# Residual of an attention block added by TensorE and evicted by ScalarE, in a fused attention and state-space kernel

## The chip, the cores and the metric

The kernel runs on one NeuronCore of one Trainium2 chip. The metric is the device time of one execution in microseconds (us). Before the change three runs gave 9474.05, 9482.28 and 9482.04 us, with a median of 9482.04 us. The profiled execution is a further one, with a time of its own.

The engines are TensorE (PE in the profile; PEld is its weight load), VectorE (DVE), ScalarE (ACT), GpSimd (POOL) and SyncE, whose queue (SP) issues nearly all transfers.

## The reference, cut to what matters

The input `x` has 8 images of 256 channels and 48 x 48 = 2304 positions. Two layers follow each other, both with a residual:

```python
# layer 0: attention over the 16 most similar positions
feat, pos = split(groupnorm(x)_tokens @ W.T + bias)          # 256 and 256 columns
pos = pos / max(norm(pos), 1e-12)
sim = pos @ pos.T                                            # 2304 x 2304 per image
topksim, topkid = top_k(sim, 16)
out = sum_k softmax(topksim)_k * feat[topkid_k]
x = x + out

# layer 1: two stacked selective scans ("mamba", depth 2) over the 2304 positions
for i in range(2):
    xn = layernorm(h);  xi, z = split(xn @ in_w.T)           # 512 and 512
    xc = silu(causal_conv4(xi));  dt, B, C = projections(xc)
    h_t = h_{t-1} * exp(dt_t * A) + dt_t * B_t * xc_t        # 512 channels x 16 states
    y = (sum over states of h_t * C_t + xc * D) * silu(z)
    h = y @ out_w.T
x = x + h
```

The change concerns the line `x = x + out` of layer 0, and the order of the work around it.

## The kernel before, in words

All arithmetic is in 32-bit floats. The program's order on each engine is the order in which the Python code emits instructions: it is written by hand, in timetables, and each engine works through its own list in that order.

**The scan sets the clock.** Layer 1 cuts an image into 6 chunks of 384 positions; 6 chunks x 2 depths make 12 *units* per image, 96 in all. A unit has 16 *steps* (32 channels each), and a step two halves of two states, so 32 halves per unit and 3072 in all. The main loop at the end of the function runs over these halves, `m`. In each half ScalarE makes the next half's decays (`decay`, L917, two exponentials into one of two PSUM banks), and VectorE runs the recurrence as one scan instruction (`run_scan`, L932). Every second half GpSimd forms the scan's input two steps ahead (`make_bx`, L893), and multiplies the states of the step before by C (`pool_part`, L960).

**SHARE** says for each half whether GpSimd ("G") or VectorE ("V", an extra product at L934) multiplies the states by C. It has three rows: row 0 for units 1 to 9 of an image, row 1 for units 0, 10 and 11, row 2 for the last image. A half marked V writes its states into the PSUM bank, and ScalarE saves the last state (`carry`, L948).

**Timetables.** Everything else of a unit stands in tables of (place, function, arguments), where place counts halves from the unit's start. Functions of the table `between` are emitted ahead of the half's scan, those of `behind` after it. These two serve units 1 to 9, `between_spare` and `behind_spare` units 0, 10 and 11, and a third pair the last image. Which pair serves an entry is decided by where the entry's place falls.

**Attention rides along.** While image b is scanned, the attention of image b+1 is emitted a piece per half, behind everything else (`ahead.go`). Only the first image's attention runs alone, ahead of the scan. Attention works on 18 blocks of 128 rows. A block follows the table `within`, with a new block every 16 halves: products `similar` (L444), copies to SBUF (`keep_similar`, L453), the four top-16 passes of VectorE (`top`), masked weights turned by TensorE and exponentiated (L495 to L504), the weighted sum (`weigh`, L515), its division (`average`, L522), a transposition back to channels (`turn_back`, L531), and the residual (`finish`, L539). `turn_back` and `finish` stand at the same place, 24 of the block, which falls on places 14 and 30 of a unit. With every third block a chunk is complete: VectorE takes its statistics (L543) and the chunk is stored for layer 1. The chunk of `x` that the residual needs is fetched from HBM by `load_chunk` once in three blocks, at place 22, from `average`.

**PSUM.** Two tiles of two banks each hold the decays, and four banks go round for every other product (`mm`). A product that finds its bank in use waits for the reader of the bank's last content.

Of the kernel before, what the change touches and what calls it, by code (L numbers as in the profile page):

```python
# [16 lines left out]
P = 128  # L17
# [9 lines left out]
def tile_conv_preact(  # L27
# [18 lines left out]
    nc = tc.nc  # L46
# [5 lines left out]
    CB = C // P  # L52
# [4 lines left out]
    TB = T // P  # L57
# [16 lines left out]


    SHARE = (
        "GGVGGGVGGGVVGGVGGGGVGGGVGGGGGVVG",
        "GVGGGVVVGGVVGGGVVGGGVGVVGGVVGVGV",
        "VVVGVVGGGVVVGGVVGGGVGGVVVVGGGVVG",
    )  # L80
    assert N % T == 0 and N % P == 0 and T % P == 0 and NS % (J * HQ) == 0

# [4 lines left out]
    def load_chunk(pool, src, c, tag, name, bufs):  # L87
        t = pool.tile([P, CB, T], F32, tag=tag, name=name, bufs=bufs)
        nc.sync.dma_start(t, src[:, c * T : (c + 1) * T].rearrange("(k p) t -> p k t", p=P))
        return t  # L90
# [3 lines left out]
    ident = const.tile([P, P], F32, tag="ident", name="ident")  # L94
# [166 lines left out]
    def layer0(b, left, pool, ps0, alone):  # L261
# [153 lines left out]
        rows = {}  # L415
# [62 lines left out]

        def invert(t):
            nc.vector.reciprocal(blocks[t]["den"], blocks[t]["den"])  # L480

        def others(t, i):

# [35 lines left out]
        def average(t):  # L519
            row = blocks[t]  # L520
            row["o"] = pool.tile([P, C], F32, tag="o", name=f"o_{b}_{t}", bufs=more)
            nc.scalar.activation(row["o"], row["po"], AF.Identity, scale=row["den"])  # L522
            if t % TB == 0:
                tag, bufs = ("xr", 2) if alone else ("x", 3)
                rows[t // TB] = load_chunk(pool, x[b], t // TB, tag, f"xr_{b}_{t}", bufs)

        def turn_back(t):
            row = blocks[t]
            row["pr"] = mm0(C, f"pr_{b}_{t}")
            for cb in range(CB):  # L530
                nc.tensor.transpose(  # L531
                    row["pr"][:, cb * P : (cb + 1) * P], row["o"][:, cb * P : (cb + 1) * P], ident
                )

        def finish(t):
            row = blocks[t]
            c, j = divmod(t, TB)
            xr = rows[c][:, :, j * P : (j + 1) * P]
            nc.vector.tensor_add(xr, xr, row["pr"].rearrange("p (k t) -> p k t", k=CB))  # L539
            if j + 1 == TB:  # L540
                xr = rows.pop(c)
                for cb in range(CB):
                    nc.vector.bn_stats(st1[:, cb, c, :], xr[:, cb, :])  # L543
                nc.sync.dma_start(x1[:, c * T : (c + 1) * T].rearrange("(k p) t -> p k t", p=P), xr)
            row.clear()
# [307 lines left out]
    def silu_z(unit):  # L853
# [3 lines left out]
        for e in range(DB - 1):  # L857
# [11 lines left out]
             dt=[], dt_d={}, dtx_d={}, dtr={}, dtxr={}, bx={}, y={}, inw={}, dmat={}, taps={}, xi={}, cv={},  # L869
# [131 lines left out]
    def leave(unit, cb):  # L1001
# [21 lines left out]
        (23, load_rep, "dt", 14), (5, load_rep, "dt", 5), (-4, load_bc, 1), (38, out_proj, 1), (17, load_d, 2),  # L1023
        (-17, tap, 1), (18, load_rep, "dtx", 13), (-8, times_x, 1), (21, gate, 1), (-22, normal),
        (1, load_rep, "dt", 3), (0, load_rep, "dtx", 4), (15, load_rep, "dt", 10), (6, load_rep, "dtx", 7),
        (10, load_rep, "dtx", 9), (11, gate, 0), (-29, spread_root), (-20, tap, 0), (-3, times_x, 3),
        (-19, load_in, 5), (33, load_out), (-3, load_rep, "dt", 0), (8, load_rep, "dtx", 8), (-22, load_in, 0),
        (21, load_rep, "dt", 13), (-10, step_size, 1), (9, copy_z, 2), (-18, in_proj, 2),
        (2, load_rep, "dtx", 5), (-21, load_in, 1), (10, sum_states, 0), (13, load_rep, "dt", 9), (9, silu_z),
        (7, load_rep, "dt", 6), (19, load_rep, "dt", 12), (-13, x_proj), (-6, load_rep, "dtx", 1),  # L1030
        (-14, load_in, 7), (-30, root), (9, load_rep, "dt", 7), (-24, load_in, 3), (17, load_rep, "dt", 11),
        (14, load_rep, "dtx", 11), (8, copy_z, 1), (-17, load_in, 6), (-3, load_d, 0), (4, load_rep, "dtx", 6),
        (-4, load_rep, "dtx", 2), (-42, load_v),
    ]
    behind = [
        (-12, split), (3, in_proj, 4), (-10, step_size, 0), (-8, load_rep, "dtx", 0), (-15, tap, 3),
        (-1, load_rep, "dt", 2), (-28, scale), (16, load_rep, "dtx", 12), (-35, square),
        (11, load_rep, "dt", 8), (8, in_proj, 6), (17, sum_states, 1), (-14, silu_x), (28, load_rep, "dt", 15),
        (-39, affine), (2, times_x, 2), (7, copy_z, 0), (19, load_rep, "dtx", 14), (10, load_rep, "dtx", 10),
        (-17, tap, 2), (-10, softplus), (-16, in_proj, 3), (36, gate, 3), (3, load_rep, "dt", 4),  # L1040
        (-3, load_rep, "dt", 1), (-29, load_in, 2), (5, in_proj, 7), (-15, taps, 1), (-2, load_rep, "dtx", 3),
        (38, leave, 1), (22, load_rep, "dtx", 15), (-8, load_in, 4), (29, load_d, 3), (-37, mean),
        (-19, taps, 0), (5, load_d, 1), (-19, in_proj, 1), (-10, load_bc, 0), (-30, root_end),
        (-9, times_x, 0), (29, gate, 2),
    ]
    between_spare = [
        (25, sum_states, 2), (-34, variance), (-21, in_proj, 0), (38, out_proj, 0), (-15, taps, 2),
        (-35, square), (39, leave, 0), (23, load_rep, "dt", 14), (5, load_rep, "dt", 5),
        (-1, load_rep, "dt", 2), (-4, load_bc, 1), (-7, times_x, 3), (38, out_proj, 1), (17, load_d, 2),
        (-17, tap, 1), (-8, times_x, 1), (19, gate, 1), (9, load_rep, "dtx", 8), (1, load_rep, "dt", 3),  # L1050
        (0, load_rep, "dtx", 4), (14, load_rep, "dt", 10), (6, load_rep, "dtx", 7), (11, load_rep, "dtx", 9),
        (-18, taps, 0), (12, load_rep, "dtx", 10), (17, load_rep, "dtx", 14), (11, gate, 0), (-1, times_x, 2),
        (-19, load_in, 5), (33, load_out), (3, load_rep, "dt", 4), (18, load_rep, "dtx", 13),
        (-22, load_in, 0), (29, load_d, 3), (21, load_rep, "dt", 13), (-20, tap, 0), (-10, step_size, 1),
        (-5, load_rep, "dt", 0), (9, copy_z, 2), (-18, in_proj, 2), (2, load_rep, "dtx", 5),
        (10, sum_states, 0), (13, load_rep, "dt", 9), (31, gate, 2), (9, silu_z), (7, load_rep, "dt", 6),
        (19, load_rep, "dt", 12), (-6, load_rep, "dtx", 1), (-14, load_in, 7), (37, gate, 3), (-31, root),
        (9, load_rep, "dt", 7), (5, load_d, 1), (-24, load_in, 3), (17, load_rep, "dt", 11),
        (14, load_rep, "dtx", 11), (-13, x_proj), (-17, load_in, 6), (-3, load_d, 0), (4, load_rep, "dtx", 6),
        (-4, load_rep, "dtx", 2), (-42, load_v), (-29, spread_root),  # L1060
    ]
    behind_spare = [
        (40, leave, 1), (-12, split), (-14, taps, 3), (-3, load_rep, "dt", 1), (4, in_proj, 4),
        (-10, step_size, 0), (-8, load_rep, "dtx", 0), (-15, tap, 3), (16, load_rep, "dtx", 12),
        (11, load_rep, "dt", 8), (8, in_proj, 6), (17, sum_states, 1), (-14, silu_x), (25, load_rep, "dt", 15),
        (-39, affine), (6, copy_z, 0), (-17, tap, 2), (-10, softplus), (-16, in_proj, 3), (7, in_proj, 5),
        (-27, load_in, 2), (6, in_proj, 7), (-15, taps, 1), (-2, load_rep, "dtx", 3), (8, copy_z, 1),
        (22, load_rep, "dtx", 15), (-16, load_in, 4), (-38, mean), (-22, normal), (-37, center),
        (-21, in_proj, 1), (-12, load_bc, 0), (33, sum_states, 3), (-30, root_end), (-9, times_x, 0),
        (-25, load_in, 1), (-28, scale),  # L1070
    ]
    between_last = [
# [74 lines left out]
    for m in range(first, PARTS * NSTEP - HOOKS + last + 1):  # L1147
        n, p = divmod(m, PARTS)
# [59 lines left out]
```

## Time and profile before

| | |
|---|---|
| median of three runs | 9482.04 us |
| profiled execution: its time, its span | 9470.14 us, 9468.4 us |
| first scan starts (first image's attention ends) | 469.7 us |
| scan of images 0 to 6, each | 1140.6 to 1143.7 us |
| scan of the last image, with what follows | 987.4 us |
| granted TensorE clock, mean | 0.899 |

The image times are differences between the starts of every 384th scan instruction in the trace. In the profile a row names the source line, engine and operation, the tiles it writes and reads, its shape and count, then the busy time, the mean of one instruction, and the idle time of the engine just before them with what ended it. A wait "A <- B" says that A's engine sat idle until B was done.

### The profile page before, as it was taken

The numbers are of one execution on the slowest core, as the hardware profiler recorded it, in microseconds if no ns is written. First come the engines' busy times: TensorE is split into PE (matmuls) and PEld (weight loads), VectorE is DVE, ScalarE is ACT, GpSimd is POOL, SyncE is SP. The second block draws the span as 40 slices with busy tenths as digits, with TensorE's granted clock in tenths as the row PEclk, the third lists the DMA queues.
The fourth block names the chain that finished last, engine by engine and source line by source line (L and its number), as shares of the span: only waits on it lengthen the run. The fifth ranks groups of instructions, "written<-read, shape, count | busy, mean of one in ns | idle before, by whom it ended". The sixth has DMA issues, their size and how long they took to land.

```text
span 9468.4 us, 120581 instructions
## 1 busy us (share of the span) xinstructions
PE 7913.3 (84%) x37049; PEld 4429.9 (47%) x37049; DVE 8866.0 (94%) x7543; ACT 7297.1 (77%) x16042; POOL 8906.1 (94%) x3985
## 2 busy tenths in 40 slices
PE   8888987888878888788878888788887889877666
PEld 6744544454544554445444545444554445433332
DVE  6599998999989999899998999999999999989999
ACT  4578887778777877787878788778877888767776
POOL 2199999999999999999999999999999999999999
PEclk9989998899988998889988999889998999977887
DMA  4134444444444444444444434444444344444443
GB/s 127 47 126 135 133 136 148 130 136 137 136 147 131 130 141 132 149 128 139 130 143 137 138 128 138 140 141 131 139 133 154 126 139 130 137 154 145 149 146 125
DMA packets 1029829, 1275.92 MB, mean 135 GB/s; under 512 B 106528, under 2 KB 998944, under 8 KB 1028416
## 3 DMA queue, kind: packets, MB, share of 16 engines
q1 hardware_dynamic: 1028640, 1268.21, 41.4%
q8 instruction: 296, 4.85, 0.2%
q14 instruction: 349, 2.86, 0.1%
q10 hardware_dynamic: 544, 0.00, 0.0%
HBM read 1050.77 MB, written 217.06 MB: 134 GB/s over the span
## 4 chain that ended last, share of the span: by engine, by line
DVE 58%; ACT 12%; issue 11%; PE 11%; POOL 4%; DMA 2%; SPq 0%; DVEq 0%; POOLq 0%; ACTq 0%
DVE bx L932 21%; DVE da L932 13%; ACT da L917 5%; DVE xc L791 5%; DVE bx L934 4%; DVE top L470 4%; DVE top L465 3%; DVE left L472 3%; POOL bx L893 2%; DVE left L468 2%; PE pe L686 2%; PE y L978 2%; POOL bx L960 2%; PE pw L996 1%; DVE z L984 1%
## 5 line engine op out<-in xcount | busy, mean ns | idle before, releaser
L893 POOL TENSOR_TENSOR bx<-BC,dtxr 128x1536 f32<-128x1536 f32 x1536 | 5299.8, 3456 | 36.5 <-PE y L978 31.3
L917 ACT ACTIVATE da<-dtr,A_sb 128x385 f32<-128x385 f32 x6144 | 3592.7, 585 | 887.7 <-DVE bx L932 574.4
L932 DVE TENSOR_TENSOR_SCAN bx<-da,bx 128x770 f32<-128x770 f32 x1986 | 3417.5, 1745 | 129.0 <-ACT da L917 84.3
L960 POOL TENSOR_TENSOR bx<-bx,BC 128x1536 f32<-128x1536 f32 (+1 forms) x1317 | 3225.8, 2449 | 62.4 <-DVE bx L932 61.4
L932 DVE TENSOR_TENSOR_SCAN da<-da,bx 128x770 f32<-128x770 f32 x1086 | 1903.7, 1753 | 114.9 <-ACT da L917 108.6
L515 PE MATMUL po<-feat,aT 128*128 128x256 f32 x5184 | 1383.6, 416 | 229.0 <-ACT dt L830 93.2
L686 PE MATMUL pe<-vn,inw 128*128 128x384 f32 (+1 forms) x2976 | 1183.3, 526 | 202.7 <-ACT vn L763 86.0
L978 PE MATMUL y<-bx,sel 128*32 128x384 f32 x12288 | 1244.4, 531 | 94.6 <-POOL bx L960 90.2
L515 PEld LDWEIGHTS po<-feat,aT 128*128 128x128 f32 x5184 | 1027.4, 206 | 632.2 <-ACT aT L504 182.9
L444 PE MATMUL psim<-pos 128*128 128x512 f32 x2520 | 1182.3, 611 | 119.3 <-DVE xc L791 64.2
L934 DVE TENSOR_TENSOR bx<-da,BC 128x768 f32<-128x768 f32 x1086 | 1040.4, 958 | 37.4
L686 PEld LDWEIGHTS pe<-vn,inw 128*128 128x128 f32 x2976 | 562.1, 200 | 642.3 <-ACT vn L763 107.5
L978 PEld LDWEIGHTS y<-bx,sel 128*32 128x32 f32 x12288 | 398.0, 117 | 915.1 <-issue 701.0
L444 PEld LDWEIGHTS psim<-pos 128*128 128x128 f32 x2520 | 497.0, 207 | 694.0 <-issue 363.3
L791 DVE SCALAR_TENSOR_TENSOR xc<-pe,cw,xc 128x384 f32<-128x384 f32 x1080 | 653.9, 611 | 33.3 <-ACT xc L782 8.0
L504 ACT ACTIVATE aT<-pt 128x512 f32<-128x512 f32 (+1 forms) x720 | 387.5, 547 | 332.0 <-PE pt L496 329.8
L996 PE MATMUL pw<-z,ow 128*128 128x384 f32 x1536 | 549.2, 504 | 71.6 <-ACT aT L504 38.5
L495 PE MATMUL pt<-ident,sim 128*128 128x128 f32 x2592 | 537.0, 288 | 15.6 <-DVE v L750 7.2
L948 ACT COPY h_st<-da 128x2 f32<-128x2 f32 x884 | 139.5, 158 | 489.4 <-DVE bx L934 479.3
L975 PE MATMUL y<-xc,dmat 128*128 128x384 f32 x768 | 385.6, 588 | 153.2 <-ACT dt L830 37.6
L487 ACT ACTIVATE rest<-left,three 128x512 bf16<-128x512 f32 (+1 forms) x720 | 453.4, 669 | 63.7 <-DVE left L472 63.7
L496 PE MATMUL pt<-minus,rest 128*128 128x128 bf16 x2592 | 494.7, 224 | 2.8 <-ACT rest L487 2.8
(160 smaller groups left out, 9989.7 us busy)
## 6 DMA issues: line engine op xcount, KB each, us to landing
dtxr<-dtx_d SPq DMA_DIRECT2D x1536, 192.0 KB, 2.8
dtr<-dt_d SPq DMA_DIRECT2D x1536, 192.0 KB, 2.7
BC<-bc_d SPq DMA_DIRECT2D x192, 768.0 KB, 5.3
inw<-in_in_wT_dram SPq DMA_DIRECT2D x744, 128.0 KB, 2.5
dtx_d<-dtx SPq DMA_DIRECT2D x384, 192.0 KB, 1.9
dt_d<-dt SPq DMA_DIRECT2D x384, 192.0 KB, 2.0
ow<-in_out_wT_dram SPq DMA_DIRECT2D x96, 512.0 KB, 4.6
dmat<-diag SPq DMA_DIRECT2D x384, 64.0 KB, 2.5
```

The source lines that it names most:

```text
L444: nc.tensor.matmul(pm, pos[:, k, t * P : (t + 1) * P], pos[:, k, c0 : c0 + w], start=(k == 0), stop=(k == CB - 1),)
L495: nc.tensor.transpose(pt[:, q], row["sim"][:, r], ident)
L515: nc.tensor.matmul(row["po"], aT[:, m % PT, :], feat[:, m, :], start=(m == 0), stop=(m == NB - 1))
L686: nc.tensor.matmul(pe, w[:, k], unit["vn"][:, k, lo:], start=(k == 0), stop=(k == CB - 1))
L791: nc.vector.scalar_tensor_tensor(unit["xc"][e], unit["pe"][e][:, k : k + T], cw[:, unit["d"], e, k : k + 1], unit["xc"][e], ALU.mult, ALU.add,
L893: nc.gpsimd.tensor_tensor(bx[:, :, 1:], unit["BC"][0], unit["dtxr"][i].unsqueeze(1).to_broadcast([P, Q, T]), ALU.mult,)
L917: nc.scalar.activation(da[:, s * (1 + T) : (s + 1) * (1 + T)], unit["dtr"][i], AF.Exp, scale=A_sb[:, unit["d"], i, p * HQ + s : p * HQ + s ...
L932: nc.vector.tensor_tensor_scan(h, da, g, 0.0, ALU.mult, ALU.add)
L934: nc.vector.tensor_tensor(bx[:, :, 0:T], da.rearrange("p (q t) -> p q t", q=HQ)[:, :, 1:], unit["BC"][1][:, qs], ALU.mult,)
L960: nc.gpsimd.tensor_tensor(g[:, :, 0:T], g[:, :, 1:], unit["BC"][1][:, qs], ALU.mult)
L978: nc.tensor.matmul(y[j * G : (j + 1) * G, :], sel, unit["bx"][k * J + j][:, q, 0:T], start=False, stop=True, skip_group_check=True,)
L996: nc.tensor.matmul(pw, unit["ow"][:, k, cb * P : (cb + 1) * P], unit["z"][k], start=(k == 0), stop=(k == DB - 1),)
```

## The change: what it does

1. `turn_back` issues, after each of its two transpositions, a product of the identity with the matching 128 x 128 piece of `x`, which accumulates onto the transposed piece in PSUM.
2. `finish` no longer adds on VectorE. ScalarE copies the sum from PSUM to SBUF, over the piece of `x` that was read. The statistics and the store are as before.
3. The fetch of the chunk of `x` moves from `average` (place 22) to `invert` (place 12), since TensorE now needs it at place 24.
4. SHARE: rows 0 and 1 keep their counts of G and V in each row and move some of them; row 2 likewise.
5. Some entries of the tables for units 1 to 9 and for units 0, 10 and 11 move. One of them is the fetch of the step-size rows of step 12 in the spare table, from place 19 to 17. The tile it fills is the one from which the second half of step 9 takes its decays; that half is emitted one place later, so it now waits for this transfer and reads what it brought.

```diff
     SHARE = (
-        "GGVGGGVGGGVVGGVGGGGVGGGVGGGGGVVG",
-        "GVGGGVVVGGVVGGGVVGGGVGVVGGVVGVGV",
-        "VVVGVVGGGVVVGGVVGGGVGGVVVVGGGVVG",
+        "GGVGGGVGGGVVGVGGGGGVGGGVGGGGGVVG",
+        "GVGGGVVVGGVVGGGGVGGVGGVVVGVVGVGV",
+        "VVGGVVGGGVVVGGVVGGGVGGVVGVGVGVVV",
     )
...
         def invert(t):
             nc.vector.reciprocal(blocks[t]["den"], blocks[t]["den"])
+            if t % TB == 0:
+                tag, bufs = ("xr", 2) if alone else ("x", 3)
+                rows[t // TB] = load_chunk(pool, x[b], t // TB, tag, f"xr_{b}_{t}", bufs)
...
             nc.scalar.activation(row["o"], row["po"], AF.Identity, scale=row["den"])
-            if t % TB == 0:
-                tag, bufs = ("xr", 2) if alone else ("x", 3)
-                rows[t // TB] = load_chunk(pool, x[b], t // TB, tag, f"xr_{b}_{t}", bufs)
...
                 nc.tensor.transpose(
                     row["pr"][:, cb * P : (cb + 1) * P], row["o"][:, cb * P : (cb + 1) * P], ident
                 )
+                nc.tensor.matmul(
+                    row["pr"][:, cb * P : (cb + 1) * P], ident,
+                    rows[t // TB][:, cb, t % TB * P : (t % TB + 1) * P],
+                    start=False, stop=True, skip_group_check=True,
+                )
...
-            nc.vector.tensor_add(xr, xr, row["pr"].rearrange("p (k t) -> p k t", k=CB))
+            nc.scalar.copy(xr, row["pr"].rearrange("p (k t) -> p k t", k=CB))
```

The moves in the tables, entry by entry (old place and table, new place and table):

| entry | before | after |
|---|---|---|
| `tap 0` | -20 between | -20 behind |
| `load_in 5` | -19 between | -27 behind |
| `load_d 3` | 29 behind | 31 between |
| `sum_states 3` | 33 behind_spare | 35 between_spare |
| `load_rep dt 12` | 19 between_spare | 17 between_spare |
| `load_rep dtx 6` | 4 between_spare | 4 behind_spare |
| `in_proj 7` | 6 behind_spare | 7 behind_spare |

## The prediction

> **What bounds the kernel now.** I first read the page's busy shares and its chain of waits.
>
> ```profile
> PE 7913.3 (84%) x37049; PEld 4429.9 (47%) x37049; DVE 8866.0 (94%) x7543; ACT 7297.1 (77%) x16042; POOL 8906.1 (94%) x3985
> DVE 58%; ACT 12%; issue 11%; PE 11%; POOL 4%; DMA 2%; SPq 0%; DVEq 0%; POOLq 0%; ACTq 0%
> ```
>
> VectorE and GpSimd are equally full, and the chain runs mostly over VectorE. An average hides the stages, so next I asked for busy time by stretch: in image 3's scan unit 0, units 1 to 9, units 10 and 11, then the last image.
>
> ```profile
> core 0: us, PE busy (x) PEld busy (x) DVE busy (x) ACT busy (x) POOL busy (x), PEclk, DMA share, GB/s
> 3899.95:3995.50 95.55, 77.26 (x357) 42.87 (x358) 84.66 (x76) 74.21 (x161) 90.30 (x67) 0.88 0.44 143
> 3995.50:4856.90 861.40, 760.22 (x3612) 428.59 (x3610) 848.11 (x708) 693.18 (x1536) 854.53 (x334) 0.93 0.41 133
> 4856.90:5043.30 186.40, 139.47 (x624) 73.71 (x623) 163.30 (x146) 140.78 (x302) 175.93 (x87) 0.82 0.46 150
> 8468.80:9456.00 987.20, 685.48 (x2866) 321.12 (x2866) 927.72 (x757) 727.10 (x1595) 977.02 (x387) 0.80 0.43 142
> ```
>
> In units 1 to 9, where the attention blocks ride along, GpSimd is busy 854.5 of 861.4 us and VectorE 848.1. Both bound this stage: VectorE leaves 13 us per image, GpSimd 6.9. In the last image GpSimd alone is full. Who GpSimd waits for, from the first scan on:
>
> ```profile
> POOL bx L960 <- DVE bx L932: 61.4, 106, 1.8
> POOL bx L893 <- PE y L978: 31.3, 39, 1.8
> ```
>
> Placed by unit, the wait for VectorE is 28.0 us in units 1 to 9 of the seven images, 23.8 in units 0, 10 and 11, and 9.6 in the last image; the wait for TensorE is 15.7 in the first and 15.4 in the second. These waits are all that a faster VectorE or TensorE can give back.
>
> **What the Trainium skill says.** "Perfetto Trace Analysis", section "Identifying Performance Opportunities", advises work on the most-contended engine, by occupancy. Here two share that place and the change relieves one, so the other's slack is the ceiling. "PSUM — Partial Sum Buffer", section "Engine vs sequencer instructions", says that the queues of ScalarE, VectorE and GpSimd are strict FIFO and that matmuls start and complete in program order. The trace agrees: in the stretch below everything stands in listed order. "VectorE: DVE Perf Modes", section "The TRN2 errata", prices a PSUM-to-SBUF copy on ScalarE at 172 + 256 cycles at 1.2 GHz, an estimate of 0.357 us; the trace has 0.365 for the same shape, which I use.
>
> **The change part by part.** The rows for the operations that go, come, or resemble those that come:
>
> ```profile
> L539 DVE TENSOR_TENSOR xr<-xr,pr 128x256 f32<-128x256 f32 x144 | 59.1, 411 | 21.9 <-PE pr L531 21.5
> L372 ACT COPY feat<-pf 128x256 f32<-128x256 f32 x144 | 52.1, 365 | 4.8 <-PE pf L345 4.5
> L232 PE MATMUL lb<-ident,rs 128*128 128x128 f32 x576 | 92.1, 297 | 22.5 <-DVE rs L184 22.3 <-PE y L978 0.3
> ```
>
> *VectorE's addition goes.* 144 times 0.411 is 59.1 us. The 18 of the first image lie off the path (see below), and so does the 21.9 us wait for `pr`, all of it there. The other 126 are worth 51.8 us, 7.4 per image.
>
> *Identity products come.* The program has 288. The like-shaped 288 products at L232 left 576 records, two each, and 92.1 us. So one costs 0.32 us, a block 0.64, and the whole 92 us on TensorE, which has 16% free. Below nothing is excluded (no work leaves TensorE); the upper bound is the latency, 2 x 2 x 0.297 = 1.2 us per block.
>
> *ScalarE's copy comes*: 144 x 0.365 = 52.6 us on an engine that is 77% busy. It stands in ScalarE's queue ahead of `keep_similar` (the copy at L453) and the next decays, so it matters when `pr` is ready. A block at place 14 of unit 4:
>
> ```profile
> 4326.77 0.38 PE L531 MATMUL pr<-ident,o 128*128 128x128 f32 x2
> 4327.05 0.18 ACT L907 COPY bx<-h_st 128x4 f32<-128x4 f32 x1
> 4327.13 0.57 ACT L453 COPY sim<-psim 128x512 f32<-128x512 f32 x1
> 4328.72 0.41 DVE L539 TENSOR_TENSOR xr<-xr,pr 128x256 f32<-128x256 f32 x1
> 4328.84 0.16 ACT L948 COPY h_st<-da 128x2 f32<-128x2 f32 x1 [1.13 <-DVE bx L934]
> 4329.16 1.02 DVE L543 BATCH_NORM_STATS2 st<-xr 128x6 f32<-128x384 f32 x2
> ```
>
> ScalarE reaches the new copy at 4327.23. `pr`, ready at 4327.15, becomes ready at 4327.79. The copy ends at 4328.2, the L453 copy at 4328.8, and the 1.13 us in which ScalarE waited for VectorE have absorbed both. The statistics, due at 4328.8 on VectorE, no longer follow their own engine's addition but wait for a copy that is 0.6 us old. Over all 63 blocks at place 14 ScalarE has 1.02 us of idle before its next decay and needs 0.5 + 0.37; in 14 of them it has under 0.1, and there I expect up to 0.4 us lost, 6 us in all. At place 30 `pr` has been ready for 3.7 us and only the copy counts, against 1.36 us of idle. Behind the copy the L453 copy frees a bank for `similar`: TensorE waited 0.61 us there and now starts 1.1 us later, ahead of a later wait of 1.78 us for VectorE that covers it.
>
> *SHARE.* Each row keeps its counts, and GpSimd's sum per unit with them (8 double products of 3.19 us and 7 single of 1.69 in row 0). In row 0 the double moves from step 6 to 7: GpSimd reaches step 7 earlier by 1.5 us and waits there for VectorE (slack now 0.1 to 2.3 us), and in return does not wait at step 13 (0.5 us in most units). Zero, within 3 us per image either way. In the last image step 15 has no GpSimd product any more: it was the last of the program, 1.7 us after a 1.73 us wait. Minus 1.
>
> *Table moves.* The step-12 rows: transfer 2.7 us plus some 0.3 of issue after the decay that it overwrites, against 2.2 us at which the next decay now starts: 0.8 us late. VectorE's scan comes 4.26 us after that decay's end, which hides it; uncovered it would be 21 x 0.8 = 17 us. `sum_states 3` two places later spares TensorE a wait for GpSimd of 4.5 us in unit 11 and 1.2 in unit 10; VectorE waits 2.25 us behind the first. I take 0.6 per image, minus 4 (0 to -16). `load_in 5` fills its slot earlier, so `load_in 1` waits for `in_proj 0`: 2.5 us of transfer against 3.0 to 3.9 us between the two products in most units, and a stall of 2.8 in unit 1 that TensorE's 15 us of slack there take. The fetch of `x`, ten halves (30 us) earlier on SP, lands long before TensorE needs it; SP's other moves pass a transfer or two. Zero.
>
> *First image alone.* Here TensorE is full (133 of 140 us busy from 200 to 340) and the chain goes top passes, `rest`, `pr`, next `psim`, its copy, next top pass. VectorE's addition is not on it; TensorE's 0.64 is, 18 times: plus 11 (0 to 22).
>
> *Sum.* VectorE offers 51.8 us and GpSimd's waits cap what comes out: in units 1 to 9 all 28.0 for VectorE and a part (2) of TensorE's, in units 10 and 11 some 10 of 39, as VectorE arrives there ahead. That is -40. With +11, -4 and -1: -34. The profiled execution took 9470.1 us (span 9468.4 plus 1.7), so 9436; the median of the runs lies 11.9 above it, so **9448**.
>
> **The rivals.** *GpSimd's floor holds* (no change): its waits only change their name, from VectorE to TensorE, which has 92 us more to do just ahead of the `y` sums at places 17 and 18. For it: 99.2% busy. Against: VectorE's lead over its input is 5 us and more, so it can run ahead. Then -10 in units 1 to 9, +11 at the start, -5 for the moves: 9478. *All of it comes out*: the 51.8 in full and most of the 39 us of waits in units 0, 10, 11 (25): -77 + 11 - 5 gives 9411. For it: VectorE's gaps in units 1 to 9 are 13 us per image, most of them its own short ones. Against: in unit 3 it already waits 1.8 us for a memset of GpSimd (L905), which ties the two together once per image. *ScalarE is held at the copy* (slower): `pr` comes later than reckoned and the decays behind it are late. It decides from about 1.1 us after ScalarE's arrival at place 14. With products at twice the price, `pr` is 1.1 late, need 1.5 against 1.0: 63 x 0.5 = 32, start +23, the short ones +6, `y` sums late by 0.6 in 63 units +38, against -40 - 5: +54, 9536. The change does take the instruction off VectorE; that it does nothing is excluded.
>
> **How the numbers follow.** A measurement of this kernel tells 0.2% (19 us) from no change. Forecast 0.48, its own range 9426 to 9463; all of it 0.14; floor 0.23; held 0.15. Faster is the first two, 0.62; same 0.23; slower 0.15. The range leaves out the held case's upper part and the best end: 9398 to 9495.
>
> **What would show it.** Right: no L539 on VectorE, a copy of 0.37 us, product records near 0.16; POOL's wait for L932 below 35 us; images near 1138 us, the start near 480. Wrong: ScalarE waiting for `pr` over 60 us in total, more DVE waits for `da`, or POOL's wait for `y` above 50.

## The result and the profile after

The changed kernel took **9436.93 us** (median, 9433.71 to 9438.63) against 9479.24 (9474.05 to 9482.28) for the kernel before beside it: a ratio of 0.9958, 95% interval 0.9944 to 0.9973. It is faster by 42 us, more than the 0.2% that a measurement can tell; the forecast was 9448, 34 us below the 9482.04 of the first three runs. The profiled execution's span fell by 36.4 us, from 9468.4 to 9432.0; 34 us was the forecast for it, too. The total is close to the forecast. Where the time came from is not what the forecast said, and most of what follows is about that.

The page's busy line, and the same stretches of image 3 and the last image as before (scan unit 0, units 1 to 9, units 10 and 11, then the last image):

```profile
PE 7932.2 (84%) x37625; PEld 4491.6 (48%) x37625; DVE 8819.3 (94%) x7399; ACT 7325.7 (78%) x16186; POOL 8902.6 (94%) x3985
```

```profile
core 0: us, PE busy (x) PEld busy (x) DVE busy (x) ACT busy (x) POOL busy (x), PEclk, DMA share, GB/s
3879.99:3976.61 96.62, 81.98 (x367) 47.54 (x367) 84.72 (x75) 75.58 (x164) 90.78 (x67) 0.84 0.44 141
3976.61:4838.23 861.62, 760.13 (x3678) 431.55 (x3676) 842.85 (x691) 696.18 (x1553) 852.66 (x333) 0.94 0.42 133
4838.23:5020.03 181.80, 136.08 (x619) 72.58 (x619) 162.86 (x145) 139.35 (x302) 176.74 (x88) 0.84 0.47 154
8431.63:9418.80 987.17, 674.43 (x2864) 315.27 (x2865) 927.98 (x756) 727.32 (x1595) 977.71 (x388) 0.81 0.44 142
```

VectorE lost 46.7 us of busy time in the whole program, and in units 1 to 9 of this image 5.3 us. But that stretch is as long as it was: 861.62 us against 861.40. What became shorter is units 10 and 11, 181.80 us against 186.40, where hardly an addition was removed: of the 126 of images 0 to 6, 119 stood in units 1 to 9 and 7 in unit 10.

GpSimd's waits from the first scan on, in the order of their size (engine and line, who it waited for: us in total, times, longest):

```profile
POOL bx L965 <- DVE bx L937: 45.8, 45, 2.8
...
POOL bx L898 <- PE y L983: 14.5, 7, 2.6
POOL bx L965 <- ACT xc L787: 8.2, 8, 1.9
```

(L965 is L960 of before, L898 L893, L983 L978, the scan L937 L932.) The wait for VectorE fell from 61.4 us to 45.8, but it is split in a new way: in units 1 to 9 it rose from 28.0 to 36.1, and in units 0, 10 and 11 it fell from 23.8 to 2.3. The wait of L841 for `dt`, 12.1 us before, is gone.

The new operations, as rows of the groups by form (line, engine, operation, tiles, shape and count; busy and mean ns; idle before and its releaser):

```profile
L534 PE MATMUL pr<-xr,ident 128*128 128x128 f32 x576 | 103.6, 275 | 0.0
L544 ACT COPY xr<-pr 128x256 f32<-128x256 f32 x144 | 52.6, 365 | 47.4 <-PE pr L534 47.4
```

Each product left two records, as foreseen, 0.36 us together in this row where 0.32 was taken (what a product costs on the path comes with e7), and the copy costs the 0.365 us of its model. The block at place 14 of unit 4 in image 3, the one shown of before, in order of time:

```profile
4307.09 1.75 DVE L937 TENSOR_TENSOR_SCAN bx<-da,bx 128x770 f32<-128x770 f32 x1
...
4307.79 0.39 PE L534 MATMUL pr<-xr,ident 128*128 128x128 f32 x2
4308.21 0.37 ACT L544 COPY xr<-pr 128x256 f32<-128x256 f32 x1 [0.78 <-PE pr L534]
4308.48 0.59 ACT L453 COPY sim<-psim 128x512 f32<-128x512 f32 x1
...
4308.76 0.99 DVE L548 BATCH_NORM_STATS2 st<-xr 128x6 f32<-128x384 f32 x2
4308.96 1.22 ACT L922 ACTIVATE da<-dtr,A_sb 128x385 f32<-128x385 f32 x2
```

ScalarE stood still 0.78 us for the products. VectorE came out of its scan and took the statistics without a wait; the next decay started after the two copies.

To compare kernels by stage, the table gives, from the starts of the scan instructions in each profiled execution: the first scan's start; the mean per image over images 0 to 6 of units 1 to 9, and of units 0, 10 and 11 together; and the last image from its first scan to the end of its last. The experiments follow in the rows below.

| kernel | span | start | units 1-9 | units 0, 10, 11 | last image |
|---|---|---|---|---|---|
| before | 9468.4 | 469.7 | 861.2 | 281.5 | 987.4 |
| after | 9432.0 | 473.4 | 859.1 | 277.8 | 987.2 |
| e1: residual alone | 9459.7 | 477.4 | 858.3 | 281.9 | 987.3 |
| e2: SHARE and tables alone | 9437.9 | 467.5 | 861.6 | 277.1 | 987.8 |
| e3: after, old SHARE | 9459.7 | 474.4 | 859.3 | 281.6 | 986.6 |
| e4: after, old tables | 9436.2 | 473.3 | 860.9 | 276.4 | 989.8 |
| e5: before, new row 1 of SHARE | 9429.7 | 471.9 | 860.3 | 276.5 | 988.1 |
| e6: residual and new row 1 | 9415.4 | 474.4 | 858.1 | 276.5 | 986.4 |
| e7: after, products doubled | 9447.7 | 485.3 | 860.1 | 277.2 | 988.0 |
| e8: after, `finish` a half later | 9471.0 | 475.1 | 861.3 | 280.8 | 988.2 |
| e9: before, row 1, steps 7 and 9 | 9434.5 | 466.8 | 860.8 | 277.7 | 986.3 |
| e10: before, row 1, steps 10 and 12 | 9458.2 | 467.0 | 861.1 | 280.5 | 987.5 |
| e11: before, new row 0 | 9475.0 | 470.2 | 861.8 | 281.8 | 987.5 |
| e12: e6 and another row 0 | 9467.0 | 477.9 | 864.6 | 276.7 | 987.3 |

How far such figures scatter shows where kernels share a stage's code. Before, e5, e9 and e10 share that of units 1 to 9 and differ there by up to 0.9 us per image; the start scatters by 5 us among kernels with the same first image. The column of units 0, 10 and 11 falls into two groups: 280.5 to 281.9 and 276.4 to 277.8. Every kernel of the second group has the exchange of steps 7 and 9 in row 1; of those in the first, only e8 has it. The granted TensorE clock (its mean share of full speed) does not explain the order: it is 0.899 before, 0.904 after and 0.905 in e6, but 0.908 in e8, which is as slow as before.

### The profile page after: what moved, and what is told of

Read it like the earlier page. It is cut to its first block, busy times and chain, and to the rows that moved or that the text cites. A ratio compares the mean times of both kernels' runs of the same rounds, so it can differ in the third digit from the quotient of the medians.

```text
span 9432.0 us, 121761 instructions
## 1 busy us (share of the span) xinstructions
PE 7932.2 (84%) x37625; PEld 4491.6 (48%) x37625; DVE 8819.3 (94%) x7399; ACT 7325.7 (78%) x16186; POOL 8902.6 (94%) x3985
## 5 line engine op out<-in xcount | busy, mean ns | idle before, releaser
L898 POOL TENSOR_TENSOR bx<-BC,dtxr 128x1536 f32<-128x1536 f32 x1536 | 5312.2, 3464 | 16.6 <-PE y L983 14.5
L937 DVE TENSOR_TENSOR_SCAN bx<-da,bx 128x770 f32<-128x770 f32 x1986 | 3422.0, 1746 | 116.2 <-ACT da L922 78.9
L965 POOL TENSOR_TENSOR bx<-bx,BC 128x1536 f32<-128x1536 f32 (+1 forms) x1317 | 3236.4, 2457 | 54.7 <-DVE bx L937 45.8
L937 DVE TENSOR_TENSOR_SCAN da<-da,bx 128x770 f32<-128x770 f32 x1086 | 1903.9, 1753 | 126.3 <-ACT da L922 108.4
L983 PE MATMUL y<-bx,sel 128*32 128x384 f32 x12288 | 1258.9, 534 | 84.3 <-POOL bx L965 78.9
L691 PE MATMUL pe<-vn,inw 128*128 128x384 f32 (+1 forms) x2976 | 1149.8, 515 | 186.3 <-ACT vn L768 84.0
L444 PE MATMUL psim<-pos 128*128 128x512 f32 x2520 | 1155.9, 601 | 82.8 <-DVE xc L796 41.4
L983 PEld LDWEIGHTS y<-bx,sel 128*32 128x32 f32 x12288 | 416.7, 118 | 900.2 <-issue 680.1
L826 PE MATMUL pd<-dbl,dtp_sb 16*128 16x384 f32 x768 | 363.6, 616 | 148.5 <-DVE z L989 70.5
```

Of the source, the lines that this page charges most:

```text
L444: nc.tensor.matmul(pm, pos[:, k, t * P : (t + 1) * P], pos[:, k, c0 : c0 + w], start=(k == 0), stop=(k == CB - 1),)
L691: nc.tensor.matmul(pe, w[:, k], unit["vn"][:, k, lo:], start=(k == 0), stop=(k == CB - 1))
L898: nc.gpsimd.tensor_tensor(bx[:, :, 1:], unit["BC"][0], unit["dtxr"][i].unsqueeze(1).to_broadcast([P, Q, T]), ALU.mult,)
L937: nc.vector.tensor_tensor_scan(h, da, g, 0.0, ALU.mult, ALU.add)
L965: nc.gpsimd.tensor_tensor(g[:, :, 0:T], g[:, :, 1:], unit["BC"][1][:, qs], ALU.mult)
L983: nc.tensor.matmul(y[j * G : (j + 1) * G, :], sel, unit["bx"][k * J + j][:, q, 0:T], start=False, stop=True, skip_group_check=True,)
```

## The experiments

### The halves of the change

The diff has three separable parts: the residual's new way (parts 1 to 3 of the change), SHARE, and the tables. Theory A, near that of the prediction: VectorE's removed addition is what pays in units 1 to 9, the tables pay in units 10 and 11, and SHARE only costs. Rival B: the addition's removal is the whole gain. Rival C: the new orders are.

**e1, the residual alone**: the identity products, ScalarE's copy and the earlier fetch, with SHARE and tables of before.

> Parts 1 to 3 of the change alone; SHARE and all tables as before. Theory A (the addition's removal pays in units 1 to 9, the table moves pay in units 10 and 11, and the new row 0 of SHARE takes part of the first gain back as a wait at step 7): units 1 to 9 together near 856.5 us per image against 861.3 before and 859.1 in the changed kernel, units 0, 10 and 11 within 1 us of 281.5 before, the start plus 4, so 27 to 32 us faster than before in all. Rival B (all of the gain is the addition's removal, the orders do nothing): units 0, 10 and 11 near 277.8 as in the changed kernel, 42 us faster in all. Rival C (the orders alone pay): within 10 us of before.

**e2, the orders alone**: SHARE and tables of after, with the residual added on VectorE as before.

> SHARE and the tables as in the changed kernel, the residual added by VectorE as before. Theory A: units 0, 10 and 11 near 277.8 us per image (3.7 less than before), units 1 to 9 longer than the 861.3 of before by 1 to 3 us because of the wait at step 7, so between 5 and 20 us faster than before. Rival B: within 5 us of before. Rival C: 42 us faster, the whole gain.

**e3, after with the old SHARE**, and **e4, after with the old tables**.

> The changed kernel with the three rows of SHARE as before. Theory A: GpSimd's wait for VectorE at step 7 (36 us in units 1 to 9 now) falls below 15, units 1 to 9 near 856.5 us, units 0, 10 and 11 near 278 to 280, so 5 to 18 us faster than the changed kernel. Rival: the two rows only exchange one wait for another, units 1 to 9 at 859, and the time is within 5 us of the changed kernel.

> The changed kernel with all tables as before, SHARE new. Theory A: units 1 to 9 at 859 us as in the changed kernel, units 0, 10 and 11 back near 281, so some 20 us slower than the changed kernel and 20 faster than before. Rival (units 10 and 11 gain because VectorE arrives there ahead, or through row 1 of SHARE): units 0, 10 and 11 stay near 278 and the time is within 6 us of the changed kernel.

Measured, medians against 9475.53 for before: e1 9457.58, ratio 0.9982 (0.9975 to 0.9989); e2 9441.67, 0.9967 (0.9955 to 0.9979); e3 9459.29, 0.9983 (0.9976 to 0.9990); e4 9435.18, 0.9957 (0.9940 to 0.9973).

Theory A falls in its split, and B and C, which leave one half with nothing, fall too. The residual alone gives 18 us, not 27 to 32. The orders alone give 34 us where theory A allowed at most 20, and taking the new SHARE out of the changed kernel (e3) costs 22 us instead of gaining. The tables do nothing that these runs can tell: e4 stands where the changed kernel stands, as its rival had it, and e3, which has the tables, where e1 stands, which does not. So the two halves are the residual and SHARE. The early fetch of step 12's rows, because of which the second half of step 9 reads the wrong rows, is among the tables: e1, e4, e5 and e6 are without it and read the right ones, so no gain rests on it.

GpSimd's waits in e1 show how little the residual changes for it. They are to be held against the lines of before, 61.4 us for VectorE, 31.3 for `y` and 12.1 for `dt`:

```profile
POOL bx L965 <- DVE bx L937: 44.9, 100, 2.0
...
POOL bx L898 <- PE y L983: 30.0, 35, 2.5
POOL dtx L846 <- ACT dt L835: 12.0, 13, 1.3
```

By stage, of the 28.0 us for VectorE in units 1 to 9 17.2 remain, of the 15.7 for `y` 13.3. In units 0, 10 and 11 all of GpSimd's waits together went from 109.9 to 106.9 us: nothing comes out there.

Where VectorE's time went can be read from its own side. In image 3 its busy time in units 1 to 9 fell by 5.73 us (848.11 to 842.38), over the seven images by 39.0. Its waits in that stage, over the seven images, rose from 51.6 us to some 70: for the decays from 19.5 to some 28, for the output product `pw` from 17.7 to 20.2, for GpSimd's memset (L905, now L910) from 13.4 to 16.0, and 3.2 us for a transfer that it had not waited for. The stage became shorter by 2.9 us per image, 20 us. Half of what VectorE offered went into its own waits for others, half came out.

### Which row of SHARE

Four sub-questions, each with one row or one exchange put into the kernel before.

```diff
 e5: row 1 (units 0, 10, 11), all of it
-        "GVGGGVVVGGVVGGGVVGGGVGVVGGVVGVGV",
+        "GVGGGVVVGGVVGGGGVGGVGGVVVGVVGVGV",
 e9: of it only steps 7 (GV to GG) and 9 (GG to GV)
+        "GVGGGVVVGGVVGGGGVGGVVGVVGGVVGVGV",
 e10: of it only steps 10 (VG to GG) and 12 (GG to VG)
+        "GVGGGVVVGGVVGGGVVGGGGGVVVGVVGVGV",
 e11: row 0 (units 1 to 9)
-        "GGVGGGVGGGVVGGVGGGGVGGGVGGGGGVVG",
+        "GGVGGGVGGGVVGVGGGGGVGGGVGGGGGVVG",
```

> The kernel before with row 1 of SHARE alone as in the changed kernel (the row of units 0, 10 and 11). Theory (row 1 is the whole gain of the orders: it takes 1.5 us of GpSimd work away from steps 9 and 12, where GpSimd waited for VectorE, and puts it at steps 7 and 10, where it ran late): units 0, 10 and 11 near 277 us per image against 281.5, units 1 to 9 at 861 as before, the time 25 to 33 us below before. Rival (rows 0 and 2 carry a part): less than 20 us below before.

> The kernel before; of row 1 of SHARE only the exchange between steps 7 and 9 (second half of step 7 to GpSimd, second half of step 9 to VectorE). Theory (row 1 pays where GpSimd waited for VectorE, at steps 8 and 9 of units 10, 11 and 0): this exchange is most of row 1's gain, units 0, 10 and 11 near 278 us per image and the time 20 to 35 us below before; GpSimd's wait for VectorE there falls from 24 to below 10 us. Rival (the gain comes with steps 10 and 12, where ScalarE's softplus and table loads stand): less than 12 us below before.

> The kernel before; of row 1 only the exchange between steps 10 and 12 (first half of step 10 to GpSimd, first half of step 12 to VectorE). Theory: 5 to 15 us below before, the wait for VectorE at steps 8 and 9 as before. Rival: 25 to 40 us below before, the whole of row 1's gain; GpSimd's wait for ScalarE's step sizes (12 us before) gone.

> The kernel before; row 0 of SHARE alone as in the changed kernel (a product moved from step 6 to 7 in units 1 to 9). Theory (moving GpSimd's work later makes it wait at step 7): GpSimd's wait for VectorE in units 1 to 9 rises from 28 us to 50 or more, units 1 to 9 are 0.5 to 1.5 us longer per image, the time 3 to 12 us above before. Rival (it exchanges one wait for another): within 3 us of before in those units.

Measured: e5 9428.96 against 9471.57, 0.9953 (0.9938 to 0.9968); against 9476.34, e9 9442.62, 0.9964 (0.9951 to 0.9977), e10 9464.98, 0.9988 (0.9981 to 0.9995), e11 9476.95, 1.0002 (0.9993 to 1.0010).

One row of 32 letters, which leaves all counts of G and V as they are, is worth 43 us, as much as the whole change. Of the 43 us, 35 are in units 0, 10 and 11 (5.0 us per image), to which this row applies; the rest is of the size of the scatter. Alone, the exchange of steps 7 and 9 brings 34 us, that of 10 and 12 11. Row 0 brings nothing.

How steps 7 and 9 do it can be seen in unit 10 of image 3. First GpSimd, then VectorE, of the kernel before (start, us, engine, line, instruction, and in brackets the idle time and its releaser):

```profile
4901.76 1.67 POOL L960 TENSOR_TENSOR bx<-bx,BC 128x768 f32<-128x768 f32 x1
4903.39 3.45 POOL L893 TENSOR_TENSOR bx<-BC,dtxr 128x1536 f32<-128x1536 f32 x1
4908.40 1.68 POOL L960 TENSOR_TENSOR bx<-bx,BC 128x768 f32<-128x768 f32 x1 [1.56 <-DVE bx L932]
...
4912.41 3.43 POOL L893 TENSOR_TENSOR bx<-BC,dtxr 128x1536 f32<-128x1536 f32 x1 [1.62 <-PE y L978]
4915.79 3.17 POOL L960 TENSOR_TENSOR bx<-bx,BC 128x1536 f32<-128x1536 f32 x1
```

```profile
4895.96 1.76 DVE L932 TENSOR_TENSOR_SCAN bx<-da,bx 128x770 f32<-128x770 f32 x1 [0.23 <-ACT da L917]
...
4899.00 1.75 DVE L932 TENSOR_TENSOR_SCAN da<-da,bx 128x770 f32<-128x770 f32 x1
4900.79 0.96 DVE L934 TENSOR_TENSOR bx<-da,BC 128x768 f32<-128x768 f32 x1
...
4904.68 1.91 DVE L791 SCALAR_TENSOR_TENSOR xc<-pe,cw,xc 128x384 f32<-128x384 f32 x3
4906.51 1.75 DVE L932 TENSOR_TENSOR_SCAN bx<-da,bx 128x770 f32<-128x770 f32 x1
```

The short GpSimd product at 4901.76 is step 7's: it starts 4.0 us after the scan that it needs, the one that ends at 4897.72. With step 8's, at 4908.40, the lead has turned round: GpSimd has 1.56 us with nothing to do until VectorE's scan, which ends at 4908.26. The same stretch in e5:

```profile
4880.25 3.17 POOL L960 TENSOR_TENSOR bx<-bx,BC 128x1536 f32<-128x1536 f32 x1
4883.38 3.47 POOL L893 TENSOR_TENSOR bx<-BC,dtxr 128x1536 f32<-128x1536 f32 x1
4886.80 1.68 POOL L960 TENSOR_TENSOR bx<-bx,BC 128x768 f32<-128x768 f32 x1
...
4890.45 3.45 POOL L893 TENSOR_TENSOR bx<-BC,dtxr 128x1536 f32<-128x1536 f32 x1 [1.27 <-PE y L978]
4893.84 1.69 POOL L960 TENSOR_TENSOR bx<-bx,BC 128x768 f32<-128x768 f32 x1
```

Step 7 is now double, 3.17 us, and step 8 follows with no wait. The 1.5 us of work that were added fill the 1.56 us in which GpSimd stood idle, and step 9, which is single now, is 1.5 us shorter. VectorE's product of 0.96 us at 4900.79, the second half of step 7, is gone from ahead of the scan that step 8 needs. From the product of step 7 to the end of that of step 9, 17.20 us before (4901.76 to 4918.96) became 15.28 (4880.25 to 4895.53). Over all of units 0, 10 and 11 GpSimd's wait for VectorE is 23.8 us before: 10.6 at step 8 of unit 10, 11.0 at step 9, nearly all in units 0 and 11, and 2.2 at step 10. It is 8.7 in e9, all at step 10, and gone in e5. In e10 the wait for `dt`, 12.1 us, is gone instead: step 10 has a double product there, and L841, which waited, stands behind it.

Row 0 shows the same lever with no gain. GpSimd's waits in e11, over the whole scan:

```profile
POOL bx L960 <- DVE bx L932: 86.1, 90, 2.4
...
POOL bx L893 <- PE y L978: 19.2, 13, 2.5
```

In units 1 to 9 the wait for VectorE doubles, 28.0 to 54.3 us, and the one for `y` shrinks from 15.7 to 1.1. In image 3 it is step 7, to which the double product moved, that waits: 1.0 to 2.1 us in units 1, 3, 4, 6 and 8. The prediction named this wait and the relief for it at step 13, where GpSimd waits 16.5 us in all before and not at all in e11; the 6.3 us at step 6 are gone as well. What is waited for changes, and the time hardly does. The residual then shortens this wait: with the new rows it is 57.0 us in e2, where VectorE still adds, and 36.1 in the changed kernel.

### The two gains together

**e6** has the residual of e1 and row 1 of e5, and nothing else of the change.

> Parts 1 to 3 of the change and row 1 of SHARE; rows 0 and 2 and all tables as before. Theory (the two gains lie in different units and add up; row 0 of the changed kernel only costs): units 1 to 9 near 858.4, units 0, 10 and 11 near 277, 46 to 52 us below before and 4 to 12 below the changed kernel. Rival (what VectorE saves in units 1 to 9 and what row 1 gives both come out of the same idle time of GpSimd): as the changed kernel, within 4 us.

Measured: 9420.61 against 9471.57, 0.9946 (0.9931 to 0.9960), the fastest of all kernels here. The two gains add for the most part: the 18 us of e1 and the 43 of e5 make 61, of which 51 are there. On top of row 1 the residual brings 8 us in the medians (9428.96 to 9420.61), less than alone, though within what the intervals allow. The three stretches of image 3 take 94.52, 857.64 and 181.84 us (before 95.55, 861.40 and 186.40), and of GpSimd's waits for VectorE and for `y` least is left:

```profile
POOL bx L965 <- DVE bx L937: 33.3, 72, 1.2
...
POOL bx L898 <- PE y L983: 13.9, 29, 1.5
```

Its profiled execution is 16.6 us shorter than that of the changed kernel, spread over units 1 to 9 (1.0 us per image) and the short units (1.3). The intervals of the two ratios overlap, so it is likely, and not shown, that the rest of the change (row 0, row 2 and the tables) costs time.

### The price of the products and of the copy's place

**e7** issues each identity product twice, with an identity of one half, so that the result is the same.

```diff
+    nc.vector.tensor_scalar(half, ident, 0.5, None, ALU.mult)
...
+                for _ in range(2):
+                    nc.tensor.matmul(row["pr"][...], half, ..., start=False, stop=True, ...)
-                nc.tensor.matmul(row["pr"][...], ident, ..., start=False, stop=True, ...)
```

**e8** leaves the products where they are and moves `finish`, the copy with the statistics behind it, one half on, so that ScalarE does not have to stand and wait for `pr`.

```diff
-        (12, invert), (5, others, 2), (17, turn, 2), (20, turn, 3), (24, finish), (15, weights, 1),
+        (12, invert), (5, others, 2), (17, turn, 2), (20, turn, 3), (25, finish), (15, weights, 1),
```

> The changed kernel with every identity product issued twice, each with half the identity, so that the sum is the same and the product's time on TensorE is doubled (another 0.64 us per block). If ScalarE's copy is hidden as long as the sum is ready within about 1.1 us (the prediction's working): ScalarE's idle before the copy rises from 47 us to some 100, but VectorE's wait for decays in units 1 to 9 stays within 10 us of its 21, and the time rises by 5 to 15 us, most of it in the start, which goes from 473 to 478 or more. If ScalarE is already held at the copy (the rival): VectorE's wait for decays rises by 30 us or more and the time by 30 to 50.

> The changed kernel with the copy emitted one half later (place 25), the products where they are, so that ScalarE no longer meets a sum that is not ready. If the copy costs nothing where it stands: within 4 us of the changed kernel. If it holds ScalarE there: ScalarE's idle before the copy falls from 47 us to below 15, VectorE's wait for decays in units 1 to 9 falls by 5 us or more, and the time by 5 to 15.

Measured against 9471.57: e7 9441.17, 0.9967 (0.9955 to 0.9979); e8 9477.09, 1.0005 (0.9997 to 1.0014). By the ratios e7 is some 9 us slower than the changed kernel, which their intervals do not quite tell apart, and e8 some 45.

In e7 TensorE has 576 more product records, 4 per block. What they cost where nothing hides them is seen in the first image's attention. Here is the last piece of block 2 and of block 14 (counted from 0), the addition or the copy, in before, in the changed kernel and in e7:

```profile
148.98 0.42 DVE L539 TENSOR_TENSOR xr<-xr,pr 128x256 f32<-128x256 f32 x1
361.47 0.42 DVE L539 TENSOR_TENSOR xr<-xr,pr 128x256 f32<-128x256 f32 x1 [0.69 <-PE pr L531]
```

```profile
151.65 0.35 ACT L544 COPY xr<-pr 128x256 f32<-128x256 f32 x1
369.48 0.35 ACT L544 COPY xr<-pr 128x256 f32<-128x256 f32 x1
```

```profile
152.41 0.37 ACT L547 COPY xr<-pr 128x256 f32<-128x256 f32 x1
375.90 0.35 ACT L547 COPY xr<-pr 128x256 f32<-128x256 f32 x1
```

The 12 blocks between take 212.5, 217.8 and 223.5 us. All six kernels that add on VectorE agree with the first figure within 0.03 us, and all seven with the products once with the second. So the change costs 0.45 us per block here, and doubling the products 0.47: 8.0 and 8.5 us over the 18 blocks. The start of the first scan, 11.9 us later than in the changed kernel, contains the scatter of the pieces around.

Once the scan runs, VectorE's wait for the decays rises from 20.9 to 34.9 us in units 1 to 9, by more than the 10 us of the first expectation and less than the 30 of the rival. The stage rises by 1.0 us per image, hardly more than its scatter: 7 us, while the row of the products has 64 us more of busy time in the whole program. ScalarE stands longer for the products:

```profile
ACT xr L547 <- PE pr L537: 70.9, 56, 1.6
```

This is the waiting that the "held" rival spoke of, and most of what it does to ScalarE is absorbed.

In e8 the wait for the products has gone (1.3 us in the whole program), and the kernel loses all that the change had gained. The block of place 14 again:

```profile
4327.36 3.40 DVE L937 TENSOR_TENSOR_SCAN bx<-da,bx 128x770 f32<-128x770 f32 x2
...
4328.06 0.39 PE L534 MATMUL pr<-xr,ident 128*128 128x128 f32 x2
4329.15 1.20 ACT L922 ACTIVATE da<-dtr,A_sb 128x385 f32<-128x385 f32 x2 [0.95 <-DVE bx L937]
4331.50 0.36 ACT L544 COPY xr<-pr 128x256 f32<-128x256 f32 x1
...
4331.89 1.02 DVE L548 BATCH_NORM_STATS2 st<-xr 128x6 f32<-128x384 f32 x2 [1.13 <-ACT xr L544]
4331.91 0.30 PEld L444 LDWEIGHTS psim<-pos 128*128 128x128 f32 x2 [2.51 <-ACT xr L544]
```

The sum is ready at about 4328.5 and copied at 4331.50, since a decay that waits for a scan, and behind it another activation of 1.2 us (L787), stand before the copy now. VectorE waits for it 1.13 us, and the next scan stands behind the statistics; TensorE waits too, for the bank. From the first scan on:

```profile
DVE st L548 <- ACT xr L544: 36.9, 35, 1.2
```

And with the last block a half later, the group statistics of the finished sum are late as well: in units 10 and 11 GpSimd waits 31.8 us for a mean (L205) for which it did not wait before, and the units 0, 10 and 11 give back 3.0 of the 3.7 us per image that they had gained. Neither expectation had this: one put the time within 4 us of the changed kernel, the other 5 to 15 us below it. The edit moves the copy and the statistics together, so what each would cost alone is not known.

### Another row 0

Row 0 of after only exchanges waits: it moves GpSimd's work to a later step. The opposite direction is work moved to earlier steps, where GpSimd's products start late: in e6 those of steps 3 and 11 in the median some 6 and 4 us after the scans that they need, while it waits at steps 6 and 13.

```diff
 e12: e6, with in row 0 step 3 VG to GG, 6 GG to GV, 11 GV to GG, 13 GG to GV
-        "GGVGGGVGGGVVGGVGGGGVGGGVGGGGGVVG",
+        "GGVGGGGGGGVVGVVGGGGVGGGGGGGVGVVG",
```

> Parts 1 to 3 of the change, row 1 as changed, and in row 0 two products moved earlier in the unit (first half of step 3 to GpSimd, second half of step 6 to VectorE; second half of step 11 to GpSimd, second half of step 13 to VectorE), old tables. Theory (work put where GpSimd runs late and taken from where it waits shortens the stage): GpSimd's wait for VectorE in units 1 to 9 falls from 22 us to below 10, units 1 to 9 from 858.1 to about 856.5, the time 5 to 15 us below the version with the residual and row 1 (9421), so near 9410. Rival (units 1 to 9 are held by VectorE's own chain by now): GpSimd's wait falls but the stage stays at 858, within 4 us of 9421.

Measured 9464.44 against 9476.34, 0.9987 (0.9980 to 0.9994), that is 39 us slower than e6 by the ratios. GpSimd's and VectorE's waits, to be held against those of e6:

```profile
POOL bx L965 <- DVE bx L937: 40.0, 49, 1.7
POOL bx L898 <- PE y L983: 35.5, 49, 2.9
...
POOL bx L965 <- ACT xc L787: 13.9, 14, 2.3
```

```profile
DVE da L937 <- ACT da L922: 154.0, 101, 6.0
...
DVE xr L1018 <- PE pw L1001: 48.3, 23, 2.7
```

Neither the theory nor its rival held. The waits at steps 6 and 13, 10.5 and 11.7 us in units 1 to 9 of e6, are gone as intended, but step 7 now waits 29.9 us for VectorE and the 13.9 us for ScalarE's `xc` (L787), where it had not waited. That is the place behind the exchange of steps 3 and 6: GpSimd has only a single product at step 6 now and comes to step 7 before VectorE's scan is done. The wait for `y` is longer as well, and so are VectorE's for the decays and for the output product `pw` (in the rows shown, 132.9 and 22.6 us in e6). Units 1 to 9 take 864.6 us, the longest of all. The two exchanges were not tried one by one, so which of them lengthens the waits for `y` and `pw` stays open.

## Why the prediction was right, and where not

**The bound.** Right: both engines bind units 1 to 9 and their waits are what can be given back. GpSimd's busy time in units 1 to 9 of image 3 stays at 852.7 to 854.5 us in all kernels shown, and its waits make up the rest of the stage (47.4 us over seven images before, 32.3 in e1, 34.6 in e6).

**VectorE's addition, minus 40.** The mechanism was right, with the gain capped by who waits for whom, and the size was double what it should have been. In units 1 to 9 20 us came out in e1 where 30 were put (28 for VectorE, 2 for `y`); measured, 10.8 of the one and 2.4 of the other, some 2 from GpSimd's wait for ScalarE, and the last 5 from GpSimd's busy time, 0.7 us per image less, for which no run shows a reason. Between e5 and e6, which have row 1 in common, it is 16 us, and half of that goes into the longer start. Two steps failed here. The first is "VectorE offers 51.8": the 119 additions in units 1 to 9 were charged with 0.411 us each, 48.9 us, but VectorE's busy time there fell by 39.0, 0.33 us each, because the record of an addition overlaps that of the instruction before it, by 0.08 us in the mean. The second is "in units 1 to 9 all 28.0": VectorE's own waits took 19 of these 39 us. The other term, "in units 10 and 11 some 10 of 39, as VectorE arrives there ahead", measured nothing (281.9 us against 281.5 for units 0, 10 and 11): GpSimd's wait for VectorE fell by 5.4 us there, and the stage did not become shorter.

**SHARE, "zero, within 3 us per image either way".** This is the step that was most wrong: row 1 alone gives 5.0 us per image and 43 us in all (e5). The prediction argued from the row's counts, which do not change, and looked closely at row 0 alone, where the exchange of waits did come to nothing (e11: 1.0002). It had the 39 us of waits in units 0, 10 and 11 before it and asked whether a faster VectorE would remove them, but not whether moving 1.5 us of GpSimd's work to the step ahead of the wait would. The trace of before shows it: step 7's product starts 4.0 us late, and the next waits 1.56. In the Trainium skill, "Perfetto Trace Analysis", section "Identifying Performance Opportunities", first picks the engine by its occupancy, and then looks for the gaps on that engine and for what ends them. Here occupancy, the part on which the prediction drew, said little: 59 us of additions taken off an engine at 94% gave 18, and a row that leaves each engine's sum of work as it was gave 43. The gap of 1.56 us before step 8, and what ended it, shows the place.

**The start, plus 11.** Right in its mechanism, a little too large. The change costs 0.45 us per block in the first image's attention, 8.0 us in all, and doubling the products 0.47. The two prices are equal within 0.03 us, so the addition's 0.41 us was not on the path, as the prediction says. What was mis-sized is the product's price, 0.64 us per block, taken from the busy time of a like row. The scan's start was named near 480 us; it is 473.4, and 473.3 to 477.9 in the kernels with the products once.

**Products and copy.** The row of the products has 0.72 us per block where 0.64 was taken, 103.6 us in all against 92, and on the path they cost 0.47; the copy takes 0.365 us exactly. ScalarE's wait for `pr` measured 47.4 us in the whole program, under the 60 named as a sign of trouble, and VectorE waited some 8 us longer for the decays in units 1 to 9 (e1) against the 6 us given for this. The margin of 0.6 us between the copy and the statistics was smaller in the block shown, 0.18 us (4308.58 to 4308.76), but it held; moved past it in e8, the copy costs VectorE 36.9 us of waits.

**The tables, minus 4, and the tail, minus 1.** Neither can be found: e4 and after, and e3 and e1, lie within 2 us of each other, and from the end of the last scan to the end of the program 13.2 us pass, 12.3 before. The added wait of step 9's decays is there (ScalarE waits 56.3 us for step-size rows in all, 32.3 with the old tables) and hidden, as reckoned.

**The rivals.** "Floor" came near in units 1 to 9 of the changed kernel itself: with row 0 GpSimd's wait for VectorE is 36.1 us there, and 45.8 in all stages together where below 35 was named as a sign of being right, and image 3's stage did not move; over seven images 2.1 us each remain. "All of it comes out" fell with e1. "Held at the copy" had the right place and too high a price: with doubled products, which it had priced at 32 us in the decays and 38 in `y`, VectorE's wait for the decays rose by 14 us, e7 lost 7 us in units 1 to 9, and GpSimd's wait for `y` there was 2.0 us. What the design does not bear is the reverse, a sum that is ready and a copy that stands too late (e8).

So the total was right by luck, because two errors met: the residual gave 18 us (e1) where minus 40 and plus 11 make 29, and SHARE, which was put at zero, gave the 22 between e3 and the changed kernel. Images took 1136.9 us in the mean, against the 1138 named.

## What to carry to other kernels

When two engines hand work to each other, list for each handoff how late the consumer starts and whether it then waits for the producer; work that can go to either is worth most if it leaves the step that the other waits for and fills the idle time just before, and this adds no work to either engine. The list has to be made anew after each move: in e12 two waits went and a longer one came at the step between. Taking work off one of two co-limiting engines pays only as far as the other's waits for it, and its own waits for third engines take a share: here half. A copy that only has to be somewhere between producer and reader is not free to move: a half later it stood behind an instruction that waits for a scan, and the engine that reads its result waited for it.

## What was not expected of the hardware

The busy time of a row is not what its instructions cost where nothing hides them. The profile counts time in which records of one row overlap once, but time in which they overlap records of another row in both rows. The products of the changed kernel, in pairs of records between transpositions, come to 103.6 us, 0.72 us per block; the doubled form has twice the records, of the same mean length of 275 ns, and only 64 us more, 0.45 us per block:

```profile
L537 PE MATMUL pr<-xr,half 128*128 128x128 f32 x1152 | 167.9, 275 | 0.0
```

The second figure is close to the price on the path, 0.45 to 0.47 us per block. In the same way an addition of 0.41 us took only 0.33 us from VectorE's busy time when it went. A difference between two kernels gave the price here, and a row overstated it.
